# Two attention products in quarters of the TensorE array, with the projection's columns laid out by graph

## The chip, the cores and the metric

The kernel runs on one core of one Trainium2 chip. The metric is the device time of one execution in microseconds (us): the median over several runs, lower is better. "The profiled execution" is one run with the hardware profiler on; its trace gives every instruction on every engine with start and duration.

The engines are TensorE (PE in the profile; its weight loads are listed apart as PEld), VectorE (DVE), ScalarE (ACT), GpSimd (POOL) and the one that issues most loads (SP). Each works through its own queue in order.

## The reference

Two layers, each of a graph attention and a mixture of experts, on 128 graphs of 64 nodes with 256 features, all in float32:

```
x, adj: (128, 64, 256), (128, 64, 64)
for layer in (0, 1):
    h  = layernorm(x)                       # per node
    Wh = h @ W                              # 256 x 256, per node
    e  = (Wh @ a1)[:, :, None] + (Wh @ a2)[:, None, :]     # 64 x 64 per graph
    if layer == 1: e = where(e > 0, e, 0.2 * e)
    att = softmax(where(adj > 0, e, -9e15), axis=-1)
    x  = x + elu(att @ Wh)                  # att is 64 x 64, Wh 64 x 256, per graph
    x  = x + moe(layernorm(x))              # 8 experts, each node goes to 2
```

The attention never crosses from one graph to another. What the change touches is how `e` and `att @ Wh` are formed.

## The kernel before

**Blocks.** The 8192 nodes are cut into 16 blocks of 512 rows. A block is 4 tiles (`TT`) of 128 rows, and a tile holds 2 graphs of 64 nodes (`NG`) on the 128 partitions. There are 16 blocks in each of the two layers, so the attention, the generator `attend` (L303 to L423), runs 32 times.

**One block's attention.** Layer norm is applied by ScalarE (`xn`, L278). TensorE transposes `xn` into two PSUM tiles (`pt`, L289), which go to SBUF as `xt`. For each of the 4 tiles TensorE multiplies `xt` with the weights (`pw`, L334, 258 columns: 256 of `Wh` and the two scores `Wh @ a1`, `Wh @ a2`), and ScalarE copies the result to `wh` (L345). VectorE spreads the second score on a diagonal (`sm2`, L349). Then come the two products of this study:

- `pe` (L357, L358): two products of 128x128 by 128x256 into one PSUM tile. `same` is a constant 128x128 matrix with ones in the two 64x64 diagonal blocks, so that it sums `sm2` within each graph; the identity adds the first score.
- `po` (L402): for each of the 4 tiles one product of 128x128 by 128x256. The stationary side `pT` is the transposed attention, which is zero outside its two 64x64 diagonal blocks. Two tiles share one PSUM bank: tiles 0 and 1 in `po[0]`, tiles 2 and 3 in `po[1]`.

Between the two, VectorE adds the mask (L374; in layer 1 ScalarE copies `pe` out first, L368, and VectorE applies the leaky part, L371), and takes the maximum; ScalarE takes the exponentials (L380), VectorE divides (L387), TensorE transposes the 4 tiles of the attention to 64 partitions (`pp`, L391), and VectorE and ScalarE each copy one half of `pp` into one of three constant buffers `pT_bd`, which were set to zero once at the start (L170 to L172, L394, L396). After `po`, ScalarE takes `exp` of it (`ex`, L411), and VectorE forms the elu and the residual sum (L417, L420).

**PSUM.** All of `pt`, `pw`, `pe`, `pp` and `po` come from one pool with two banks in turn (tag `"a"` of `ps_c`). The router has two banks (tag `"r"`), and the experts four (tag `"hy"`).

**The experts.** `route` (L459) sorts rows into lists in DRAM by indirect DMA (L573). The experts work on slots of 256 rows read back from the lists: `px` (L878, transposes), `xT` (L883, VectorE copy), `ph` (L960), `hT` (L970, ScalarE), `py` (L993), `ys` (L1004), and an indirect DMA out (L1026, L1036).

**Order.** From block 3 on, nothing is left to a scheduler: the instructions of TensorE, VectorE, ScalarE and SyncE stand in the order in which the Python program issues them. The strings `STEPS` (L34) are that order written out by hand, one for each layer. A token advances one generator by one `yield`: `a1` is the attention of the next block, `r0` the router of the present one, `x0`, `h0`, `y0` the phases of an expert slot. The places of the `yield`s in `attend` therefore decide what stands between two of its instructions. In `po`'s loop there are four yields: after the products of `po[0]`, after its `exp`, after the products of `po[1]`, after its `exp`. In layer 0 the products of `po[0]` and `po[1]` follow each other on TensorE; in layer 1, from its second block on, the transposes `px` of an expert slot stand between them, and in its blocks 1 to 6 (counted from 0) the `ph` of that same slot comes next.

A float32 product shows in the trace as two pairs of LDWEIGHTS and MATMUL records on the same operands, one pair after the other; a transpose shows as one pair.

Of the kernel before, what the change touches and what calls it, by code (L numbers as in the profile page):

```python
# [16 lines left out]
P = 128  # L17
# [33 lines left out]
def adj_ffn_kernel(  # L51
# [89 lines left out]
    nc.gpsimd.tensor_tensor(imod, ident[:, 0:NG], ident[:, NG : 2 * NG], ALU.add)  # L141
    same = const.tile([P, P], F32, name="same")
    nc.gpsimd.memset(same, 0.0)
    for g in range(2):
        r = slice(g * NG, (g + 1) * NG)
        nc.gpsimd.memset(same[r, r], 1.0)
    nhalf = const.tile([P, TT], F32, name="nhalf")
# [21 lines left out]
    nc.gpsimd.memset(pad[:, :, META + 1 : META + 2], -1.0)  # L169
    pT_bd = [const.tile([P, TT, P], F32, name=f"pT_bd{i}") for i in range(3)]  # L170
    for t in pT_bd:
        nc.gpsimd.memset(t, 0.0)  # L172

# [107 lines left out]

    def transposed(src, tag, ptag, name, both):

        xt = work.tile([P, KD, TB], F32, tag=tag, name=f"xt_{name}", bufs=2)
        pts = []
        for k in range(KD):
            pt = ps_c.tile([P, TB], F32, tag=ptag, name=f"pt_{name}_{k}")
            for t in range(TT):
                nc.tensor.transpose(  # L289
                    pt[:, t * P : (t + 1) * P], src[:, t, k * P : (k + 1) * P], ident  # L290
                )
            pts.append(pt)
            yield
        for k, pt in enumerate(pts):
# [4 lines left out]
            else:  # L299
                nc.scalar.copy(xt[:, k, :], pt)  # L300
        return xt

    def attend(l, b, blk):  # L303
# [22 lines left out]
        yield 1  # L326
        xt = yield from transposed(xn, "xt", "a", name, l == 0 and b < FIRST)
        yield 1
        wh = work.tile([P, TT, D + 2], F32, tag="wh", name=f"wh_{name}")
        pws = []  # L330
        for t in range(TT):
# [23 lines left out]
        yield 1  # L355
        pe = ps_c.tile([P, TT, NG], F32, tag="a", name=f"pe_{name}")
        nc.tensor.matmul(pe, lhsT=same, rhs=sm2, start=True, stop=False)  # L357
        nc.tensor.matmul(  # L358
            pe,
            lhsT=ident,  # L360
            rhs=wh[:, :, D : D + 1].to_broadcast([P, TT, NG]),
            start=False,
            stop=True,
        )
        yield
        ee = work.tile([P, TT, NG], F32, tag="ee", name=f"ee_{name}")
        if l == 1:
            nc.scalar.copy(ee, pe)  # L368
        yield
        if l == 1:  # L370
            nc.vector.scalar_tensor_tensor(ee, ee, ALPHA, ee, ALU.mult, ALU.max)  # L371
            nc.vector.tensor_tensor(ee, ee, m, ALU.add)
        else:
            nc.vector.tensor_tensor(ee, pe, m, ALU.add)  # L374
        mx = small.tile([P, TT], F32, tag="emx", name=f"emx_{name}")
# [16 lines left out]
        yield  # L392
        pT = pT_bd[(NB * l + b) % 3]
        nc.vector.tensor_copy(pT[0:NG, :, 0:NG], pp[:, :, 0:NG])  # L394
        yield
        nc.scalar.copy(pT[NG:P, :, NG:P], pp[:, :, NG:P])  # L396
        yield 1
        po, ex = [], []
        for h in range(TT // 2):
            po.append(ps_c.tile([P, 2, D], F32, tag="a", name=f"po_{name}_{h}"))  # L400
            for j in range(2):
                nc.tensor.matmul(  # L402
                    po[h][:, j, :],
                    lhsT=pT[:, 2 * h + j, :],
                    rhs=wh[:, 2 * h + j, 0:D],
                    start=True,
                    stop=True,
                )
            ex.append(work.tile([P, 2, D], F32, tag="ex", name=f"ex_{name}_{h}"))
            yield  # L410
            nc.scalar.activation(ex[h], po[h], AF.Exp)  # L411
            yield 1 if h == TT // 2 - 1 else None
        xb = work.tile([P, TT, D], F32, tag="xb", name=f"xb_{name}")
        blk["xb"] = xb
        rs = [slice(2 * h, 2 * h + 2) for h in range(TT // 2)]
        for h, r in enumerate(rs):
# [872 lines left out]
```

## Time and profile before

| | |
|---|---|
| median of 6 runs | 1336.43 us (1333.05 to 1343.47) |
| the profiled execution | 1334.46 us, of which the instructions span 1332.7 us |
| granted TensorE clock, mean over the span | 0.955 |
| instructions in the trace | 22375 |
| MATMUL records of `pe` (L357 and L358) | 64 and 64 |
| MATMUL records of `po` (L402) | 256 |
| MATMUL records of `pp` (L391) | 128 |

How to read it: the profile page gives the busy time of each engine over the whole span, then the chain of work that ended last, followed back from the last instruction (an engine's share of that chain is the share of the span in which this engine's work was what the end waited for). The view by stages gives the busy time of each engine in stretches of the span. The timeline lists instructions by engine in order of time, those of one line merged: start, time covered, engine, line, output and inputs, the array's rows and columns in use (`128*128`), the moving side (`128x256`), and the count. A MATMUL's end is modelled (its pipeline included), so the time that one really takes of TensorE is read from the distance between the starts of neighbours, not from the duration.

### The profile page before, as it was taken

What the parts mean: (1) busy time and instruction counts of PE and PEld (TensorE: products, weight loads), DVE (VectorE), ACT (ScalarE), POOL (GpSimd) and SP (SyncE); (2) the same over time, 40 slices, a digit from 0 to 9 for tenths busy, and PEclk for the clock granted to TensorE, in tenths of its full rate; (3) what the DMA queues carried; (4) which work ended last, traced back from release to release, by engine and by line L of the source; (5) the groups of instructions that cost most, each with busy time, mean ns of one, the idle gap of its engine ahead of it and who ended that gap; (6) DMA issues with size and microseconds to landing.
All of it is one profiled execution on the core that took longest, in us unless ns stands there. A gap on an engine that the chain in (4) does not pass through costs nothing.

```text
span 1332.7 us, 22375 instructions
## 1 busy us (share of the span) xinstructions
PE 1198.6 (90%) x6240; PEld 1030.7 (77%) x6240; DVE 861.6 (65%) x3477; ACT 661.2 (50%) x1562; POOL 716.8 (54%) x697
## 2 busy tenths in 40 slices
PE   6867898989888889899899899999999999988992
PEld 4655787868777777688788788888888888877981
DVE  3756777777676787888777477766677754332330
ACT  5745565656666665466454445454545453323330
POOL 4173656656655566466554565566565556533233
PEclk9868999998999999899999999999999999989996
DMA  8636667778876877899897887889988778899963
GB/s 235 207 107 195 218 209 247 223 233 261 274 222 200 290 251 252 274 294 302 280 265 212 241 254 225 234 244 277 289 243 232 179 203 243 225 271 282 276 151 35
DMA packets 275116, 311.69 MB, mean 234 GB/s; under 512 B 40615, under 2 KB 236334, under 8 KB 274992
## 3 DMA queue, kind: packets, MB, share of 16 engines
q1 hardware_dynamic: 219552, 225.02, 54.1%
q0 software_dynamic: 38544, 68.46, 20.2%
q10 hardware_dynamic: 16896, 16.78, 3.7%
q8 instruction: 50, 0.82, 0.2%
q14 instruction: 74, 0.61, 0.1%
HBM read 212.25 MB, written 99.75 MB: 234 GB/s over the span
## 4 chain that ended last, share of the span: by engine, by line
PE 58%; DVE 17%; DMA 7%; issue 4%; ACT 3%; SPq 3%; POOL 2%; POOLq 0%; DVEq 0%; ACTq 0%
PE ph_s L960 20%; PE py_s L993 18%; PE pw_g L334 7%; PE pl_r L478 3%; PE px_s L878 3%; DVE ys_s L1004 2%; PE po_g L402 2%; DMA lists<-pad 2%; DVE xT_s L883 2%; DMA out_dram<-ys_s,to_s 1%; PE pt_r L289 1%; PE pt_g L289 1%; DMA res<-ys_s,to_s 1%; ACT xn_g L278 1%; DMA wc_s<-in_w_dram 1%
## 5 line engine op out<-in xcount | busy, mean ns | idle before, releaser
L960 PE MATMUL ph_s<-xT_s,wc_s 128*128 128x256 f32 (+1 forms) x1760 | 395.9, 377 | 19.8 <-DVE xT_s L883 10.9
L993 PE MATMUL py_s<-wc_s,hT_s 128*128 128x256 f32 x1648 | 386.7, 384 | 10.1 <-ACT hT_s L970 10.0
L960 PEld LDWEIGHTS ph_s<-xT_s,wc_s 128*128 128x128 f32 x1760 | 324.8, 197 | 67.4 <-DVE xT_s L883 15.9
L573 POOL DMA_INDIRECT lists<-tn_r,ix_r x256 | 252.4, 986 | 179.8 <-issue 87.6
L993 PEld LDWEIGHTS py_s<-wc_s,hT_s 128*128 128x128 f32 x1648 | 307.3, 192 | 51.8 <-ACT hT_s L970 13.6
L1036 POOL DMA_INDIRECT out_dram<-ys_s,to_s x135 | 213.6, 1582 | 238.6 <-DMA out_dram<-ys_s,to_s 89.8
L970 ACT ACTIVATE hT_s<-ph_s,wc_s 128x256 f32<-128x256 f32 (+1 forms) x440 | 174.0, 455 | 131.8 <-PE ph_s L960 84.1
L1026 POOL DMA_INDIRECT res<-ys_s,to_s x142 | 143.2, 1008 | 61.0 <-issue 22.7
L1004 DVE TENSOR_TENSOR ys_s<-py_s,wc_s 128x512 f32<-128x512 f32 (+1 forms) x149 | 96.2, 650 | 88.3 <-PE py_s L993 75.3
L334 PE MATMUL pw_g<-gw,xt_g 128*128 128x258 f32 x512 | 128.4, 401 | 15.2 <-DVE to_s L895 7.2
L883 DVE COPY xT_s<-px_s 128x512 f32<-128x512 f32 (+1 forms) x140 | 95.1, 680 | 63.8 <-PE px_s L878 62.5
L1059 ACT ACTIVATE ys_s<-ys_s,cf_s 128x256 f32<-128x256 f32 x135 | 61.1, 500 | 140.4 <-DVE ys_s L1004 140.4
L334 PEld LDWEIGHTS pw_g<-gw,xt_g 128*128 128x128 f32 x512 | 96.9, 197 | 40.7 <-ACT wh_g L345 9.8
L278 ACT ACTIVATE xn_g<-xs,nb_g,rs_g 128x256 f32<-128x256 f32 x128 | 67.2, 591 | 103.1 <-DVE nb_g L272 103.1
L878 PE MATMUL px_s<-ident,xg_s 128*128 128x128 f32 x554 | 84.5, 277 | 8.6 <-DMA xg_s<-lists 8.6
L349 DVE TENSOR_TENSOR sm_g<-imod,wh_g 128x256 f32<-128x256 f32 x32 | 13.6, 425 | 114.3 <-ACT wh_g L345 114.2
L402 PE MATMUL po_g<-wh_g,pT_bd 128*128 128x256 f32 x256 | 73.4, 425 | 13.2 <-ACT pT_bd L396 12.5
L878 PEld LDWEIGHTS px_s<-ident,xg_s 128*128 128x128 f32 x554 | 69.4, 147 | 19.0 <-DVE hat_p_15r L710 5.2
L278 ACT ACTIVATE tn_r<-xb_g,nb_r,rs_r 128x256 f32<-128x256 f32 x128 | 66.7, 589 | 33.1 <-DVE nb_r L272 26.5
L345 ACT COPY wh_g<-pw_g 128x258 f32<-128x258 f32 x128 | 47.6, 374 | 59.3 <-PE pw_g L334 58.7
L289 PE MATMUL pt_g<-ident,xn_g 128*128 128x128 f32 x256 | 49.8, 312 | 26.3 <-ACT xn_g L278 20.5
L269 POOL TENSOR_TENSOR rs_r<-ve_r,nhalf 128x4 f32<-128x4 f32 x32 | 34.2, 1068 | 69.9 <-DVE ve_r L266 39.1
(501 smaller groups left out, 1601.8 us busy)
## 6 DMA issues: line engine op xcount, KB each, us to landing
wc_s<-in_w_dram SPq DMA_DIRECT2D x142, 512.0 KB
wc_s<-in_w_dram SPq DMA_DIRECT2D x156, 256.0 KB
xg_s<-lists SPq DMA_DIRECT2D x64, 260.0 KB
xg_s<-lists SPq DMA_DIRECT2D x64, 258.0 KB
yb<-res SPq DMA_DIRECT2D x16, 1024.0 KB
wc_s<-bcat SPq DMA_DIRECT2D x78, 129.0 KB
wc_s<-bcat SPq DMA_DIRECT2D x71, 130.0 KB
xs<-in_x_dram SPq DMA_DIRECT2D x16, 512.0 KB
```

Source lines behind the costliest of these rows:

```text
L278: nc.scalar.activation(outs(t), xb[:, t, :], AF.Identity, bias=nb[:, t : t + 1], scale=rs[:, t : t + 1])
L334: nc.tensor.matmul(pw, lhsT=xt[:, k, t * P : (t + 1) * P], rhs=gw[l][:, k, :], start=(k == 0), stop=(k == KD - 1),)
L402: nc.tensor.matmul(po[h][:, j, :], lhsT=pT[:, 2 * h + j, :], rhs=wh[:, 2 * h + j, 0:D], start=True, stop=True,)
L573: ins = pooled(f"lists{l}", lambda: nc.gpsimd.indirect_dma_start(out=lists[l], out_offset=bass.IndirectOffsetOnAxis(ap=ix[:, k, t : t + 1] ...
L878: nc.tensor.transpose(px[:, c, t * P : (t + 1) * P], xg[:, t, c * P : (c + 1) * P], ident)
L883: nc.vector.tensor_copy(xT[:, :, 0 : st * P], px[:, :, 0 : st * P])
L960: nc.tensor.matmul(ph[:, j, r], lhsT=w[:, o : o + P], rhs=xT[:, c, r], start=(c == 0), stop=(c == KD - 1),)
L970: nc.scalar.activation(hT[:, f + j, r], ph[:, j, r], AF.Gelu if l == 0 else AF.Relu, bias=w[:, OB1[l] + f + j : OB1[l] + f + j + 1],)
L993: nc.tensor.matmul(py[:, t, :], lhsT=hT[:, f, t * P : (t + 1) * P], rhs=w[:, O2[l] + f * D : O2[l] + (f + 1) * D], start=(f == 0), stop=(f ...
L1004: nc.vector.tensor_tensor(ys[:, r, :], py[:, r, :], w[:, OB2[l] : OB1[l]].unsqueeze(1).to_broadcast([P, r.stop - r.start, D]), ALU.add,)
L1026: ins = pooled(group, lambda: nc.gpsimd.indirect_dma_start(out=res[sl["part"]], out_offset=self.row(sl, t), in_=sl["ys"][:, t, :], in_offs ...
L1036: ins = pooled("sums", lambda: nc.gpsimd.indirect_dma_start(out=out, out_offset=self.row(sl, t), in_=sl["ys"][:, t, :], in_offset=None, co ...
```

## The change

`pe` and `po` are computed graph by graph, as 64x64 products, each in one quarter of the TensorE array: the row half `q` holds the contraction, the column half `j` the output partitions. For that the 64 rows of a graph must lie on the row half on which the product contracts, so the columns of `xt`, and with them the rows of `wh` and `sm2`, are laid out anew: partition half `q` and tile `2h + j` now hold graph `j` of the original tile `2h + q`. The layout is made where the transposes `pt` write to PSUM (two runs of 64 columns instead of one of 128). The outputs `pe`, `po` come back in the original layout.

- `same` and its three fills go, and `pT_bd` with its three fills; `pT` becomes an ordinary work tile of half the size.
- `pe`: 8 products of 64x64 by 64x128 in place of 2 of 128x128 by 128x256, into two PSUM tiles, one for each row half `q`.
- `po`: 8 products of 64x64 by 64x256 in place of 4 of 128x128 by 128x256, into two PSUM tiles, one for each `q`. All 8 stand ahead of the first `yield`, where before the second half stood two yields later. The number of yields is the same.
- The quarters are taken in the order (0,0), (1,1), (0,1), (1,0) of (`q`, `j`).
- What reads `pe` is cut in two: in layer 1 the copy of ScalarE, in layer 0 the mask addition of VectorE. `exp`, the elu and the sum are over tiles `q`, `q + 2` instead of `2h`, `2h + 1`, in as many instructions as before.

TensorE has 4041 matrix instructions (a float32 product counted once) after the change, against 3721; ScalarE and VectorE have 16 more each, GpSimd 6 fewer. In the hand-ordered part the only move is that of `po`'s second half to ahead of `px` in layer 1; in the first three blocks, which a scheduler orders, the quarters of `pe` and `po` stand in other orders too.

```diff
@@ constants @@
-    same = const.tile([P, P], F32, name="same")
-    nc.gpsimd.memset(same, 0.0)
-    for g in range(2):
-        r = slice(g * NG, (g + 1) * NG)
-        nc.gpsimd.memset(same[r, r], 1.0)
...
-    pT_bd = [const.tile([P, TT, P], F32, name=f"pT_bd{i}") for i in range(3)]
-    for t in pT_bd:
-        nc.gpsimd.memset(t, 0.0)
@@ transposed @@
                 nc.tensor.transpose(
-                    pt[:, t * P : (t + 1) * P], src[:, t, k * P : (k + 1) * P], ident
+                    cols(pt, t) if cols else pt[:, t * P : (t + 1) * P],
+                    src[:, t, k * P : (k + 1) * P],
+                    ident,
                 )
+    def by_graph(v, t):
+
+        return v.rearrange("p (h j q n) -> p h q j n", h=TT // 2, q=2, j=2)[:, t // 2, t % 2, :, :]
+
+    QUADS = [(0, 0), (1, 1), (0, 1), (1, 0)]
+
+    def half(q):
+        return slice(q * NG, (q + 1) * NG)
@@ attend @@
-        xt = yield from transposed(xn, "xt", "a", name, l == 0 and b < FIRST)
+        xt = yield from transposed(xn, "xt", "a", name, l == 0 and b < FIRST, by_graph)
...
-        pe = ps_c.tile([P, TT, NG], F32, tag="a", name=f"pe_{name}")
-        nc.tensor.matmul(pe, lhsT=same, rhs=sm2, start=True, stop=False)
-        nc.tensor.matmul(
-            pe,
-            lhsT=ident,
-            rhs=wh[:, :, D : D + 1].to_broadcast([P, TT, NG]),
-            start=False,
-            stop=True,
-        )
+        pe = [ps_c.tile([P, TT // 2, NG], F32, tag="a", name=f"pe_{name}_{q}") for q in range(2)]
+        for i in range(2):
+            for q, j in QUADS:
+                r = half(q)
+                nc.tensor.matmul(
+                    pe[q][half(j), :, :],
+                    lhsT=(ident if i else ones)[r, r],
+                    rhs=(
+                        wh[r, j::2, D : D + 1].to_broadcast([NG, TT // 2, NG])
+                        if i else sm2[r, j::2, :]
+                    ),
+                    start=(i == 0),
+                    stop=(i == 1),
+                )
         yield
         ee = work.tile([P, TT, NG], F32, tag="ee", name=f"ee_{name}")
         if l == 1:
-            nc.scalar.copy(ee, pe)
+            for q in range(2):
+                nc.scalar.copy(ee[:, q::2, :], pe[q])
...
-            nc.vector.tensor_tensor(ee, pe, m, ALU.add)
+            for q in range(2):
+                nc.vector.tensor_tensor(ee[:, q::2, :], pe[q], m[:, q::2, :], ALU.add)
...
-        pT = pT_bd[(NB * l + b) % 3]
-        nc.vector.tensor_copy(pT[0:NG, :, 0:NG], pp[:, :, 0:NG])
-        yield
-        nc.scalar.copy(pT[NG:P, :, NG:P], pp[:, :, NG:P])
+        pT = work.tile([P, TT // 2, P], F32, tag="pT", name=f"pT_{name}", bufs=2)
+        nc.vector.tensor_copy(pT[half(0), :, :], pp[:, 0::2, :])
+        yield
+        nc.scalar.copy(pT[half(1), :, :], pp[:, 1::2, :])
         yield 1
-        po, ex = [], []
+        po = [ps_c.tile([P, TT // 2, D], F32, tag="a", name=f"po_{name}_{q}") for q in range(2)]
+        ex = []
         for h in range(TT // 2):
-            po.append(ps_c.tile([P, 2, D], F32, tag="a", name=f"po_{name}_{h}"))
-            for j in range(2):
+            for q, j in QUADS:
                 nc.tensor.matmul(
-                    po[h][:, j, :],
-                    lhsT=pT[:, 2 * h + j, :],
-                    rhs=wh[:, 2 * h + j, 0:D],
+                    po[q][half(j), h, :],
+                    lhsT=pT[half(q), h, half(j)],
+                    rhs=wh[half(q), 2 * h + j, 0:D],
                     start=True,
                     stop=True,
                 )
-            ex.append(work.tile([P, 2, D], F32, tag="ex", name=f"ex_{name}_{h}"))
-            yield
-            nc.scalar.activation(ex[h], po[h], AF.Exp)
-            yield 1 if h == TT // 2 - 1 else None
+        yield
+        for q in range(2):
+            if q:
+                yield
+            ex.append(work.tile([P, TT // 2, D], F32, tag="ex", name=f"ex_{name}_{q}"))
+            nc.scalar.activation(ex[q], po[q], AF.Exp)
+            yield 1 if q else None
...
-        rs = [slice(2 * h, 2 * h + 2) for h in range(TT // 2)]
+        rs = [slice(q, TT, 2) for q in range(2)]
```

More of the change, by code (lines that the diff above doesn't have):

```diff
@@ L280, in ln_apply, with transposed @@
             )
-    def transposed(src, tag, ptag, name, both):
+    def transposed(src, tag, ptag, name, both, cols=None):
         xt = work.tile([P, KD, TB], F32, tag=tag, name=f"xt_{name}", bufs=2)
```

## The prediction

> **What bounds the kernel now.** I read the page first: busy times, then the chain of work that ended last.
>
> ```profile
> PE 1198.6 (90%) x6240; PEld 1030.7 (77%) x6240; DVE 861.6 (65%) x3477; ACT 661.2 (50%) x1562; POOL 716.8 (54%) x697
> ...
> PE 58%; DVE 17%; DMA 7%; issue 4%; ACT 3%; SPq 3%; POOL 2%; POOLq 0%; DVEq 0%; ACTq 0%
> ```
>
> TensorE is the bound: busy for 90% of the span and itself 58% of the chain. How tight it is where attention runs, the view by stages tells (columns: stage, its length, busy time of PE, PEld, DVE, ACT, POOL with counts, clock, DMA share, GB/s):
>
> ```profile
> 300.00:500.00 200.00, 175.60 (x942) 149.44 (x943) 145.21 (x579) 123.94 (x263) 116.51 (x116) 0.97 0.78 250
> ...
> 900.00:1100.00 200.00, 199.84 (x1059) 176.25 (x1058) 140.08 (x561) 98.27 (x255) 117.59 (x94) 1.00 0.83 237
> ```
>
> In layer 0 (first stage) TensorE is busy 88%, late in layer 1 100%. The stages between lie between these, and the mean over the 32 blocks is about 0.92. So I count 0.92 of any TensorE time that the attention gains or loses.
>
> What the two products cost comes from the distance between starts in the timeline of TensorE late in layer 1, where nothing waits:
>
> ```profile
> 1077.63 0.60 PE L357 MATMUL pe_g<-sm_g,same 128*128 128x256 f32 x2
> 1078.07 0.59 PE L358 MATMUL pe_g<-wh_g,ident 128*128 128x256 f32 x2
> 1078.50 1.89 PE L960 MATMUL ph_s<-xT_s,wc_s 128*128 128x256 f32 x8
> 1080.23 1.85 PE L478 MATMUL pl_r<-rw,xt_r 128*128 128x8 f32 x16
> 1081.93 3.70 PE L993 MATMUL py_s<-wc_s,hT_s 128*128 128x256 f32 x16
> 1085.47 0.60 PE L878 MATMUL px_s<-ident,xg_s 128*128 128x128 f32 x4
> 1085.90 0.60 PE L391 MATMUL pp_g<-ident,ee_g 128*64 128x128 f32 x4
> 1086.34 3.62 PE L993 MATMUL py_s<-wc_s,hT_s 128*128 128x256 f32 x16
> 1089.80 1.03 PE L402 MATMUL po_g<-wh_g,pT_bd 128*128 128x256 f32 x4
> 1090.66 0.60 PE L878 MATMUL px_s<-ident,xg_s 128*128 128x128 f32 x4
> 1091.10 1.03 PE L402 MATMUL po_g<-wh_g,pT_bd 128*128 128x256 f32 x4
> 1091.96 7.07 PE L960 MATMUL ph_s<-xT_s,wc_s 128*128 128x256 f32 x32
> ```
>
> Four things: `pe` takes 1078.50 - 1077.63 = 0.87 us for 4 records, and `po` twice 0.86 us for 4, so 0.215 us for a record with 256 moving columns. A record with 128 takes 0.108 (`px`, `pp`: 0.43 for 4). A record with 8 takes (1081.93 - 1080.23)/16 = 0.106: there the weight load of 128 columns is the limit. And `pp`, which uses 64 columns of the array, follows and precedes 128-column work at the same distance as any other.
>
> The last view is the start of `pe` in layer 0 after an idle stretch, with the weight loads:
>
> ```profile
> 125.46 0.30 PEld L357 LDWEIGHTS pe_g<-sm_g,same 128*128 128x128 f32 x2 [0.28 <-DVE sm_g L349]
> 125.47 0.70 PE L357 MATMUL pe_g<-sm_g,same 128*128 128x256 f32 x2
> 126.00 0.59 PE L358 MATMUL pe_g<-wh_g,ident 128*128 128x256 f32 x2
> ```
>
> Two records take 0.53 us here instead of 0.43: an uncovered load of 128 columns costs 0.10 us. Elsewhere it hides behind the record before.
>
> **The change part by part.** Before, a block pays 0.87 + 1.72 = 2.59 us for the two products, 82.9 us in 32 blocks; this is all the change can win from.
>
> *The quarter products.* After, there are 8 products in `pe` with half the moving columns and 8 in `po` with the same. A float32 product is two records, one after the other, in the same quarter, and all MATMULs in the trace start in program order. End to end that is 16 x 0.108 = 1.73 us for `pe` and 16 x 0.215 = 3.44 us for `po`: exactly twice as much. Quarter products use a quarter of the array each, so the edit only pays if several run side by side. The trace of before has none that could, so I bound it. Four abreast: 5.17/4 = 1.29 us, a gain of 1.30 us for a block (41.6 us in all). None abreast: a loss of 2.58 us (82.6 us).
>
> Between them I take what order allows. The second record of a product needs its own quarter, which the first still uses; so it waits, and the next product's first record stands behind it. Once it starts, that next record can start beside it in another quarter, and no third one can. So neighbours overlap in pairs, and n products take n + 1 record times instead of 2n: 9 x 0.108 + 9 x 0.215 = 2.91 us, already 0.32 more than before. To it comes the weight load of the next product, if it too starts only with the record ahead of it. By columns (64 of the 128 that cost 0.106) I estimate 0.053 us; the ends are 0 (hidden) and 0.106. For 7 handovers in each of `pe` and `po` that is 14 x 0.053 = 0.74 us. I keep it, since every load that follows an unfinished record in this trace hides behind one record only. Sum 3.65 us, a loss of 1.06 us for a block, 33.9 in all, and 31.2 us after the factor 0.92.
>
> *Switching between full array and quarters*, 4 times in a block: the only change of form in the trace, into and out of `pp`, costs nothing (0.43 and 0.44 us for 4 records on both sides). I take 0. The upper end is a pipeline that must run empty each time: the modelled duration of a 256-column record (median 0.379 us in the view of `po`) less its 0.215 is 0.164 us, 128 times, 21 us.
>
> *`po`'s second half ahead of `px`.* In layer 1 `px` stands between the halves, and its copy by VectorE hides behind the second half. This row is from the block shown:
>
> ```profile
> 1091.30 0.69 DVE L883 COPY xT_s<-px_s 128x512 f32<-128x512 f32 x1 [0.21 <-PE px_s L878]
> ```
>
> From the end of `px` (1091.10) to the end of the copy (1091.99) is 0.89 us, and the second half covers 0.86 of them. After, `px` comes after all of `po`, and where its own `ph` is next, in blocks 1 to 6 of layer 1, TensorE stands still for those 0.89 us: 6 x 0.89 = 5 us. In the later blocks another slot's `ph` of 16 records stands between, and it is hidden.
>
> *Readers of `pe` cut in two.* ScalarE's copies take 0.372 us for 256 columns and 0.58 for 512, so 0.27 for 128: twice that is 0.17 more, 16 times, in an engine with 50% idle in front of work that VectorE continues; 0. VectorE's mask addition takes 0.42 for 256 and 0.68 for 512 columns, so 0.29 for 128, 0.16 more, 16 times, 2.5 us on an engine that is 17% of the chain and mostly so in layer 0; I take 1 us. Without cover the two together cost 5 us.
>
> *`exp` of the first half* waits for all of `po`; ScalarE's next work that TensorE waits for is behind a later `ph`, so 0. *PSUM*: `pe` takes both `"a"` banks instead of one. Their last contents are `pw` of tiles 2 and 3, which ScalarE has read before `sm2` can start; no new wait. *Start*: six fills leave POOL (some 2 us), but its first work after them waits for a load of `adj`; 0. *Transposes in two runs of 64*: same columns, 0.
>
> *Sum*: 31.2 + 5 + 1 = 37 us on the profiled execution's 1334.5, so 1371.5; that execution is 2 us under the median of the runs, and I predict 1371 us.
>
> The Trainium skill, page "TensorEngine Tiling (Array Packing)", section "Key Properties", says that changing the tiling mode drains TensorE. For a change of columns alone the `pp` rows disagree; by the rule the result would be some 21 us later, 1392. Page "TensorE: Matmul & The Clock Gate", section "Part 3: Packing small matmuls — row/col tiling", has products in different tiles start about 4 ns apart and sixteen of them run 10.6 times as fast; by that alone four would run abreast and the result would be near 1302. No run here shows it, and it speaks of tiles, not of products of two records each.
>
> **The rivals.**
>
> *Four abreast (faster).* One mechanism: the second record of a product waits in its quarter without holding up the next quarters. Then `pe` and `po` cost 1.29 us, and 41.6 x 0.92 = 38 us go, less the 6 us of the other edits: 1302. It decides once the two products take under 2.4 us for a block. For it: the operands are independent and the outputs lie in different banks or partitions. Against it: in this trace no MATMUL ever starts before the one ahead of it in the program.
>
> *End to end (slower still).* Float32 products in quarters don't overlap at all: 82.6 x 0.95 (TensorE is then the bound nearly throughout) = 78, plus 6: 1419; with switches that run empty 1440. For it: not one pair of products in the trace runs side by side.
>
> *Pairs, all loads hidden*: 0.32 x 32 x 0.92 + 6 = 15 us, 1350; part of my forecast's own range of 1345 to 1392. *Balance*: some three abreast, whose gain the other edits eat; within 7 us of now.
>
> **How the numbers follow.** Pairs (1345 to 1392) 0.41; end to end 0.32; four abreast 0.20; balance 0.07. A change under 0.5%, 6.7 us, can't be told from none. So faster 0.20, same 0.07, slower 0.73. The range leaves out the faster case and holds the rest: 1330 to 1440.
>
> **What would show it.** The distance from the first `pe` record to what follows late in layer 1: 1.34 us for pairs, 0.43 for four abreast, 1.73 end to end (0.87 before); for `po` 2.3, 0.86 and 3.4 (1.72 before). Starts of different quarters in pairs, or all apart. A gap in front of `ph` after `px` in blocks 1 to 6 of layer 1. A gap of some 0.16 us at `pe`'s and `po`'s edges, if switching costs. The forecast is wrong if more than two records share a start, or none do.

## The result and the profile after

The change makes the kernel slightly slower: 1347.6 us (median of 20 runs, 1339.54 to 1354.73) against 1336.1 us (46 runs) on the same chip, ratio 1.0078 with a 95% interval of 1.0062 to 1.0093. Run again on another chip it gave 1.0054 (1.0036 to 1.0072). The profiled execution spans 1341.3 us, 8.6 more than before. The sign was forecast and the size was not (37 us), and the reasons turn out to be mostly others.

The page of the changed kernel, the busy times and the shares of the chain:

```profile
PE 1188.3 (89%) x6880; PEld 997.3 (74%) x6880; DVE 863.0 (64%) x3493; ACT 659.3 (49%) x1578; POOL 715.0 (53%) x691
...
PE 48%; DVE 28%; DMA 5%; ACT 5%; issue 4%; POOL 2%; SPq 1%; POOLq 0%; DVEq 0%; ACTq 0%
```

TensorE is busy 10 us less, and its share of the chain falls from 58% to 48%, while VectorE's rises from 17% to 28%. So TensorE has less to do, and the end waits for something else more often. The view by stages of the changed kernel (columns as before):

```profile
300.00:500.00 200.00, 172.32 (x1037) 143.08 (x1036) 145.48 (x576) 118.48 (x256) 115.52 (x115) 0.94 0.79 251
900.00:1100.00 200.00, 199.27 (x1182) 171.48 (x1180) 142.82 (x575) 98.92 (x262) 121.54 (x97) 1.00 0.82 238
```

In layer 0 TensorE is busy 86% instead of 88%, at a granted clock of 0.94 instead of 0.97. Late in layer 1 it is full as before. There the timeline of TensorE shows what the products cost now:

```profile
1059.40 1.09 PE L412 MATMUL po_g<-wh_g,pT_g 64*64 64x256 f32 x16
1060.42 0.66 PE L891 MATMUL px_s<-ident,xg_s 128*128 128x128 f32 x4
1060.92 7.07 PE L973 MATMUL ph_s<-xT_s,wc_s 128*128 128x256 f32 x32
...
1086.53 0.60 PE L281 MATMUL pt_r<-ident,tn_r 128*128 128x128 f32 x4
1087.06 0.45 PE L363 MATMUL pe_g<-sm_g,ones 64*64 64x128 f32 x8
1087.33 0.40 PE L363 MATMUL pe_g<-wh_g,ident 64*64 64x128 f32 x8
1087.65 1.99 PE L973 MATMUL ph_s<-xT_s,wc_s 128*128 128x256 f32 x8
1089.49 1.85 PE L491 MATMUL pl_r<-rw,xt_r 128*128 128x8 f32 x16
```

By the distance between starts, `po` takes 1060.42 - 1059.40 = 1.02 us (1.72 before) and `pe` 1087.65 - 1087.06 = 0.59 (0.87 before). This is neither pairs nor end to end: four quarters run abreast. The starts of the 16 MATMUL records of that `po`, one by one (us from the span's start):

```
1059.398  .405  .412  .418
1059.665  .672  .678  .685
1059.881  .890  .897  .901
1060.097  .105  .112  .117
```

Bunches of four, 4 to 9 ns apart, and the bunches 0.216 us apart (0.267 for the first). The semaphores in the trace tell which records these are: the first weight load of the first bunch waits for VectorE's copy of `pT` (row half 0), the second already for ScalarE's (row half 1), though in the program the second record of the first product stands between them. So the second record of a float32 product waits for its own quarter, and the products of the other quarters pass it. In block 17 one record starts 0.18 us ahead of three others, and the four records of its quarter keep that lead (535.69, 535.96, 536.17 and 536.39 us, against 535.87, 536.14, 536.35 and 536.57).

The switch between the two forms is not free. Four bunches at 0.215 would be 0.86 us, `po` takes 0.16 more; `pe`, with bunches at 0.108, also takes 0.16 more than 0.43. And the neighbours are late: `pt_r` 0.53 instead of 0.43, `ph` 1.84 instead of 1.73, `px` 0.50 instead of 0.43, and `py` ahead of `po` 3.55 instead of 3.46. Together some 0.69 us in a block, 0.17 for each of the four changes of form. (What happens inside TensorE at such a change the trace doesn't show.) What remains is (0.87 + 1.72) - (0.59 + 1.02) - 0.37 = 0.61 us a block, 20 us in 32 blocks, that TensorE wins (0.37 is what the neighbours lose). The question is where they went.

**Where it is lost and won.** I compare when `pe` of each block starts (blocks 0 to 15 are layer 0), in us after the same block in the profile of before. Single executions of one kernel differ by some 3 us here, so the table gives several: A are the profiles with quarters in both layers (the changed kernel twice), B those with layer 0 as before and quarters in layer 1, C those with quarters in layer 0 alone. They are explained below.

| kernel | block 4 | 16 | 17 | 23 | 31 |
|---|---|---|---|---|---|
| A changed | 2.3 | 6.9 | 7.6 | 13.9 | 9.4 |
| A changed, again | 3.8 | 10.1 | 8.3 | 14.4 | 10.0 |
| B layer 1 alone | 2.4 | 4.4 | 2.6 | 8.7 | 4.1 |
| C layer 0 alone | 6.2 | 7.2 | 8.0 | 8.3 | 8.4 |
| C layer 0 alone, again | 5.4 | 8.8 | 9.7 | 9.8 | 9.9 |

Three parts can be read off. Layer 0 loses some 6 us: block 16 is 8 us late on average in the four profiles with quarters there, and 2 us (-0.8 to 4.8) in the five with layer 0 as before. Blocks 17 to 22 lose 6 us, where layer 1 has quarters. And blocks 23 to 31 win 4.5 us, 0.55 in a block, close to the 0.61 on paper: there TensorE is busy all the time.

### The profile page after: what moved, and what is told of

Same layout as the page of the kernel before. It is cut to its first block, busy times and chain, and to the rows that moved or that the text cites. A ratio compares the mean times of both kernels' runs of the same rounds, so it can differ in the third digit from the quotient of the medians.

```text
span 1341.3 us, 23677 instructions
## 1 busy us (share of the span) xinstructions
PE 1188.3 (89%) x6880; PEld 997.3 (74%) x6880; DVE 863.0 (64%) x3493; ACT 659.3 (49%) x1578; POOL 715.0 (53%) x691
## 4 chain that ended last, share of the span: by engine, by line
PE 48%; DVE 28%; DMA 5%; ACT 5%; issue 4%; POOL 2%; SPq 1%; POOLq 0%; DVEq 0%; ACTq 0%
PE ph_s L973 17%; PE py_s L1006 14%; PE pw_g L337 7%; DVE ys_s L1017 3%; PE pl_r L491 3%; DVE xT_s L896 3%; DVE xs L313 2%; ACT xn_g L270 2%; PE px_s L891 2%; PE pt_g L281 2%; DVE st_g L255 2%; DVE st_r L255 2%; DMA out_dram<-ys_s,to_s 1%; DVE xb_g L433 1%; DVE xb_g L430 1%
## 5 line engine op out<-in xcount | busy, mean ns | idle before, releaser
L973 PE MATMUL ph_s<-xT_s,wc_s 128*128 128x256 f32 (+1 forms) x1760 | 402.4, 381 | 29.9 <-DVE xT_s L896 20.5
L261 POOL TENSOR_TENSOR rs_r<-ve_r,nhalf 128x4 f32<-128x4 f32 x32 | 34.2, 1068 | 72.9 <-DVE ve_r L258 37.8
L281 PEld LDWEIGHTS pt_g<-ident,xn_g 128*128 128x128 f32 x256 | 33.5, 156 | 49.1 <-ACT xn_g L270 42.0
```

Of the source, the lines that this page charges most:

```text
L281: nc.tensor.transpose(cols(pt, t) if cols else pt[:, t * P : (t + 1) * P], src[:, t, k * P : (k + 1) * P], ident,)
L973: nc.tensor.matmul(ph[:, j, r], lhsT=w[:, o : o + P], rhs=xT[:, c, r], start=(c == 0), stop=(c == KD - 1),)
```

## The experiments

The runs fell on different chips: on some the kernel before takes 1336 to 1338 us, on others 1407 to 1416. Every ratio is against the kernel before on the same chip, with its 95% interval.

### First round: what of the change costs by itself

*Kernel before with both halves of `po` ahead of the first yield* (`e1`):

```diff
                     stop=True,
                 )
+        yield
+        for h in range(TT // 2):
+            if h:
+                yield
             ex.append(work.tile([P, 2, D], F32, tag="ex", name=f"ex_{name}_{h}"))
-            yield
             nc.scalar.activation(ex[h], po[h], AF.Exp)
```

> The kernel before, with both halves of po put ahead of the first yield, so that px comes after all of po in layer 1, as in the changed kernel; full-array products as before. Theory A (the move costs: ph waits for the copy xT): 5 to 10 us slower than before (1341 to 1346), since in the changed kernel TensorE's wait in front of ph for xT rose from 10.9 to 20.5 us. Theory B (the clock: TensorE is granted half speed for 144.6 us instead of 123.0, because shorter products leave it idle more often) says no change from this edit, within 3 us. Theory C (the readers of pe cut in two cost DVE and ACT time) says no change either.

Measured: 1.0027 (0.9995 to 1.006), where the kernel before takes 1416 us. That fits the 5 us of the prediction (0.35%), but the interval does not exclude zero.

*Kernel before with the readers of `pe` cut in two* (`e2`):

```diff
-            nc.scalar.copy(ee, pe)
+            for q in range(2):
+                nc.scalar.copy(ee[:, q::2, :], pe[:, q::2, :])
...
-            nc.vector.tensor_tensor(ee, pe, m, ALU.add)
+            for q in range(2):
+                nc.vector.tensor_tensor(ee[:, q::2, :], pe[:, q::2, :], m[:, q::2, :], ALU.add)
```

> The kernel before, with the reader of pe cut in two instructions as in the changed kernel (ScalarE's copy in layer 1, VectorE's mask addition in layer 0); full-array products as before. Theory C: 3 to 5 us slower than before, 0.16 us for each of 32 blocks with nothing to cover it. Theories A and B: within 2 us of before.

Measured: 1.0049 (1.0017 to 1.0081), some 7 us: far more than the 1 us that I had put on it. This is the first surprise, and the third round takes it up.

*The changed kernel with `px` ahead of `po` in layer 1* (`e3`), a token moved in `STEPS[1]` (a part of the line):

```diff
-y1 y2 a1 x2 r0 x0 x1 a1 p R1
+y1 y2 x2 r0 x0 a1 x1 a1 p R1
```

> The changed kernel with one token moved in the order of layer 1, so that px stands ahead of po there too and the copy xT hides behind po. Theory A: 5 to 10 us faster than the changed kernel, so 1338 to 1343, about level with before, and TensorE's wait for xT in front of ph back to about 11 us. Theories B and C: within 3 us of the changed kernel's 1347.6.

Measured: 1.0186 (1.014 to 1.0232). On this chip the loss lies almost wholly in layer 0, which this edit leaves alone: block 16 starts at 579.9 us, in `e2` at 551.0, and from there to block 31 it is 609.6 us against 610.2. So the ratio says nothing of layer 1; the second round repeats the edit without quarters in layer 0.

*The changed kernel with filler products* (`e4`): one of 128x128 by 128x512 ahead of `pt` and one ahead of `po`, in blocks 4 to 22. The lines show the one ahead of `po`; the other stands in `transposed`.

```diff
+        if NB * l + b in FILL:
+            nc.tensor.matmul(po[0], lhsT=ident, rhs=gw[0][:, :, 0:D], start=True, stop=True)
```

> The changed kernel with two products added in each of blocks 4 to 22 (identity by 512 columns, 0.86 us of TensorE each), whose result is overwritten by the work that follows: one ahead of the transposes pt of the attention, one ahead of po, where TensorE waits in layer 0. Theory B: time at half clock falls from 144.6 us towards 120, and the kernel is 3 to 8 us faster than the changed one. Theories A and C: no faster; 0 to 30 us slower, by how much of the 38 products' 33 us meets an idle TensorE.

Measured: 1.0374 (1.0329 to 1.0419). Half clock means windows of 3.4 us and more in which the trace gives TensorE a granted clock of 0.5. Between blocks 4 and 16 TensorE spends 106 us in such windows instead of 133 in `e3`, and yet the stretch takes 478.8 us instead of 475.5. The kernel is not faster, as theory B had it; but the 24 fillers of this stretch are 20.6 us of work, of which only 3.3 show, so the run cannot tell what the clock is worth.

### Second round: layer by layer

A flag chooses quarters or the old form block by block; in both, the copies of `pp` go to the diagonal blocks of `pT_bd`.

```diff
+    def in_quads(l, b):
+        return l == 1
...
+        quads = in_quads(l, b)
```

The changed kernel (`e5`), quarters in layer 1 alone (`e6`), in layer 0 alone (`e7`), and in layer 1 alone with the token moved as above (`e8`):

> The changed kernel once more, so that it stands on the same chip as the other kernels of this call. Ratio to the kernel before 1.008 where the kernel before takes 1336 us, and up to 1.02 on a chip where it takes 1416. Theory A (what is lost lies where TensorE waits for other engines, layer 0 and the first blocks of layer 1; what is won lies from block 23 on): relative to the kernel before, block 16 starts about 7 us late or more, and blocks 23 to 31 win 0.5 us each. Theory B (half clock): TensorE spends some 20 us more at half clock than before.

> Quarters in layer 1 alone; layer 0 as before. Theory A (the loss of layer 0 comes from quarters where TensorE has slack, the loss of blocks 16 to 22 from the order in layer 1): block 16 level with before, blocks 16 to 22 lose some 7 us, blocks 23 to 31 win 4.5 us: 2 us slower, ratio 1.002 (0.998 to 1.006). Theory B (TensorE with less to do falls to half clock more often, all over the kernel): time at half clock as before up to block 16, so again level there, then less than 3 us lost in blocks 16 to 22. Theory R (the loss is the per-block price of the readers cut in two and of switching, alike in both layers): half of the loss of the changed kernel, ratio 1.004 to 1.01.

> Quarters in layer 0 alone; layer 1 as before. Theory A: block 16 starts as late as in the changed kernel (7 us, up to 30 on a slower chip), and the delay stays level to the end; ratio 1.005 (up to 1.02). Theory B: the same lateness, and time at half clock 15 us or more above the kernel before in the first 500 us. Theory R: half of the loss of the changed kernel. If layer 0 costs nothing here, ratio 1.000, the loss of the changed kernel is all in layer 1.

> Quarters in layer 1 alone, and there px ahead of po, so that po stands between px and the ph that waits for the copy of px. Theory A: blocks 16 to 22 lose 0 to 2 us instead of 7 and the later blocks win 4.5: ratio 0.996 (0.993 to 1.000), faster than before and than the changed kernel. Theory B: the order makes no difference, ratio as with quarters in layer 1 alone. Theory R: 1.003.

Measured, all on one chip: both layers 1.0054 (1.0036 to 1.0072); layer 1 alone 1.0004 (0.9984 to 1.0024); layer 0 alone 1.0063 (1.004 to 1.0086); layer 1 with `px` ahead 0.9975 (0.9957 to 0.9993). The parts add up, and theory A stands: the loss is in layer 0, and layer 1 is a draw of a loss and a gain. Theory R, half and half, is out. The last is the first version below both kernels, by 0.25%; run again on another chip (`e13`, below) its interval includes 1.

Why does layer 1 lose in its first blocks? One reason is the wait that was forecast. The view of TensorE's waits in the stretch from 480 to 760 us, before and after (us in total, times, longest):

```profile
PE ph_s L960 <- DVE xT_s L883: 4.3, 2, 2.6
```

```profile
PE ph_s L973 <- DVE xT_s L896: 10.0, 8, 2.7
```

That is 5.7 us more. But VectorE's queue shows that the place of `px` is only half of it. In block 17 of the kernel before, the copy `xT` stands behind the copy of `pT` and a row of small router instructions, and ends 3.2 us after that copy began:

```profile
526.32 0.41 DVE L394 COPY pT_bd<-pp_g 64x256 f32<-64x256 f32 x1
...
528.79 0.69 DVE L883 COPY xT_s<-px_s 128x512 f32<-128x512 f32 x1
```

So it does in the changed kernel (3.3), and in `e8` too (3.1), where `px` is done more than a microsecond sooner after that start. Before, `po`, `px` and `po` filled this time; now `po` is 0.7 us shorter, and what it saves becomes a wait. With `px` ahead of `po` that `ph` still waits 0.99 us, and the waits in this stretch are 7.6 us (6 times).

### Third round: the table load

The other reason is on ScalarE. Block 19 in the kernel before, ScalarE and then VectorE's maximum:

```profile
593.53 0.37 ACT L368 COPY ee_g<-pe_g 128x256 f32<-128x256 f32 x1 [0.28 <-PE pe_g L358]
593.92 1.28 ACT L380 ACT_TABLE_LOAD   x1
595.31 0.35 ACT L380 ACTIVATE ee_g<-ee_g,emx_g 128x64 f32<-128x64 f32 x1
```

```profile
594.85 0.42 DVE L376 TENSOR_REDUCE emx_g<-ee_g 128x4 f32<-128x256 f32 x1
```

The exponentials need another table in ScalarE, and its load of 1.28 us runs while VectorE adds the mask and takes the maximum. The first exponential starts 0.03 us after the maximum. The same block in the changed kernel:

```profile
603.67 0.43 ACT L377 COPY ee_g<-pe_g 128x128 f32<-128x128 f32 x2
605.67 1.28 ACT L390 ACT_TABLE_LOAD   x1 [1.57 <-DVE emx_g L386]
606.96 0.35 ACT L390 ACTIVATE ee_g<-ee_g,emx_g 128x64 f32<-128x64 f32 x1
```

```profile
605.17 0.42 DVE L386 TENSOR_REDUCE emx_g<-ee_g 128x4 f32<-128x256 f32 x1
```

Now the load itself waits for the maximum, and the first exponential starts 1.37 us after it. So it is in all of blocks 16 to 21, in all ten profiles that have the copy of `pe` cut in two without more; in the kernel before it is 0.03 to 0.04 us in blocks 17 to 21 and 0.43 in block 16. In the trace a separate semaphore wait stands ahead of the load, which the kernel before does not have: the wait that used to sit on the exponential now sits in front of its table load. From block 22 on no table is loaded there, and the exponentials start 0.09 us after the maximum.

The Trainium skill, page "ScalarE: Activation LUTs", section "What ACT_TABLE_LOAD costs", gives some 1283 ns for the load, as here, and some 1380 ns more for a drain; the rows here show no such gap, neither ahead of the load (593.92, after a copy that ends at 593.90) nor behind it (606.96, after a load that ends at 606.95).

To test it, one small exponential on a constant goes behind the copies, in blocks 0 to 5 of layer 1, so that the load comes with an instruction that waits for nothing (`e9`, and `e14` with its partner `e13`, which is `e8` again):

```diff
                 for q in range(2):
                     nc.scalar.copy(ee[:, q::2, :], pe[q])
+                if b < 6:
+                    nc.scalar.activation(early, imod[:, 0:1], AF.Exp)
```

> Quarters in layer 1 alone with px ahead of po, and in blocks 0 to 5 of layer 1 one small exp of 128x1 on a constant behind the two copies of pe, so that ScalarE's table load for exp need not stand behind the wait for the maximum. Theory T (cutting the copy of pe in two gives the exponentials one more wait, which stands ahead of the table load of 1.28 us; before, the load ran beside VectorE's mask and maximum): in the six blocks the first exp starts 0.1 to 0.3 us after the maximum, not 1.37; six times 1.1 to 1.3 us, 6 to 8 us, come back, block 23 starts level with before or earlier, and the whole takes some 1326 us where the kernel before takes 1337, ratio 0.992 (0.989 to 0.995). Rival (the loss of blocks 16 to 22 is the clock or the waits for xT): no change against the kernel without the small exp, ratio 0.9975.

> Quarters in layer 1 alone with px ahead of po, once more, as partner of the kernel with the early table load. Ratio to the kernel before 0.9975 as measured (0.996 to 0.9995).

> The same with the small exp of 128x1 behind the copies of pe in blocks 0 to 5 of layer 1. Theory T (the table load of 1.28 us behind the wait for the maximum costs 1.1 to 1.3 us in each of the six blocks): 5 to 8 us below its partner, ratio to the kernel before 0.993 where that takes 1337 us; block 23 starts 2 to 4 us earlier than in the kernel before. Rival (the table load is hidden by other waits): within 2 us of its partner.

Block 19 with the early load:

```profile
595.76 0.43 ACT L403 COPY ee_g<-pe_g 128x128 f32<-128x128 f32 x2
596.22 1.28 ACT L405 ACT_TABLE_LOAD   x1
597.51 0.20 ACT L405 ACTIVATE early<-imod 128x1 f32<-128x1 f32 x1
597.79 0.35 ACT L423 ACTIVATE ee_g<-ee_g,emx_g 128x64 f32<-128x64 f32 x1
```

The load runs beside VectorE again. `e9`: 0.9985 (0.9959 to 1.001), on a chip where the kernel before takes 1413 us. `e13`: 0.9988 (0.9963 to 1.0012); `e14`: 0.9962 (0.994 to 0.9985), a second version that is faster than before, 1332.5 us against 1337.8. Of the 5 to 8 us expected between the partners only some 2 to 4 came, and the two intervals overlap; the profiles say why. From block 17 to 23 the partner loses 3.3 us and the kernel with the early load wins 0.8: 4.1 us back in five loads. But block 16 gives 3.6 us away, so that these two profiles differ by 0.3 us from block 16 to 23. There the small exponential with its load stands in front of the copy `xt_r` (the wait of `pl` for it is 2.21 us instead of 0.71), and the `pl` and `py` behind that wait run at half clock:

```profile
484.46 3.16 PE L552 MATMUL pl_r<-rw,xt_r 128*128 128x8 f32 x14 [2.21 <-ACT xt_r L304]
487.47 3.68 PE L1067 MATMUL py_s<-wc_s,hT_s 128*128 128x256 f32 x8
```

Eight records of `py` take 3.5 us here, where they take 1.81 in the partner. That the longer wait brings on the half clock is not shown. Leaving the small exponential out of that block was not tried.

Each cut alone in the kernel before, as in `e2`:

> The kernel before with only the mask addition of layer 0 cut in two. Two additions over 128 columns take 0.13 us more than one over 256 (0.29 each against 0.42, overlapping a little): 16 times 0.13 is 2 us if all of it lies on the path, ratio 1.000 to 1.0015. If it is what layer 0 loses with quarters, 1.005.

> The kernel before with only ScalarE's copy of pe of layer 1 cut in two. Theory T: the table load comes behind the wait for the maximum in blocks 0 to 5 of layer 1, the first exp starts 1.37 us after the maximum in place of 0.03, and the kernel loses 5 to 8 us, all of it between block 16 and block 23, ratio 1.005 (1.003 to 1.006). Rival (the added 0.17 us of copy is all there is, hidden): 1.000.

Measured, on a chip where the kernel before takes 1407 us: the mask addition of layer 0 cut 0.9968 (0.9921 to 1.0014), the copy of layer 1 cut 1.0037 (0.9995 to 1.0078). The load stands behind the wait in the second and not in the first. The size in layer 1 is near the expected one, though its interval touches none; in layer 0 the cut costs nothing that shows, and more than some 2 us is outside the interval. Added, the two give 1.0005, where both together gave 1.0049 on another chip (`e2`); the intervals overlap.

### Four records of a quarter in a row

*The changed kernel with `po` ordered by quarter* (`e12`), two products of a quarter one after the other:

```diff
-        for h in range(TT // 2):
-            for q, j in QUADS:
+        for q, j in QUADS:
+            for h in range(TT // 2):
```

> The changed kernel with po's products ordered by quarter, two products of a quarter one after the other, then the next quarter. Theory of four queues (each quarter has its own, a product that waits in its quarter holds up no other, however many stand behind it): po stays at 1.02 us late in layer 1. Theory of the prediction, one product further on (whatever waits behind a product of its own quarter holds up all that follow): the second product of a quarter waits for the two records of the first, and neighbours overlap only across the change of quarter: 1.5 to 3 us. If only the second record of the same product can wait aside: some 1.9 to 2.6 us.

```profile
1060.65 1.11 PE L412 MATMUL po_g<-wh_g,pT_g 64*64 64x256 f32 x16
1061.70 0.66 PE L891 MATMUL px_s<-ident,xg_s 128*128 128x128 f32 x4
```

1061.70 - 1060.65 = 1.05 us against 1.02 (1.04 in most blocks). Four records of one quarter in a row hold up the others by next to nothing: within a bunch the starts are 10 to 16 ns apart instead of 4 to 9. So what waits for its quarter does not stand in the way of what follows: the assumption of the prediction is refuted for four records deep. Whether each quarter has a queue of its own the trace does not tell.

This kernel ran once, 1462 us on a chip where the kernel before takes 1413, so only its rows are used. One of them limits what was said of layer 1: from block 16 to 23 it takes 313.5 us, and `e9`, with `px` ahead and the early load, 287.8 on the same chip; on the faster chips the changed kernel takes 281.3 there and `e8` 277.1. So where the chip is slower, layer 1 in the changed kernel's order can lose much more than 6 us; no run separates the causes.

### Layer 0

*Quarters in blocks 4 to 15 of layer 0 alone* (`e10`), *the same with each product of `po` done twice* (`e11`), and, on another chip, *quarters in all of layer 0 with 0.86 us of filler ahead of `po`* (`e15`) beside its partner (`e16`, which is `e7` again). The three edits, in that order:

```diff
-        return l == 0
+        return l == 0 and b >= 4
...
-            for h in range(TT // 2):
+            for h in [*range(TT // 2)] * 2:
...
+            if b >= 4:
+                for _ in range(2):
+                    nc.tensor.matmul(po[0][:, 0, :], lhsT=ident, rhs=gw[0][:, 0, 0:D], start=True, stop=True)
```

> Quarters in blocks 4 to 15 of layer 0 alone. Theory S (part of the loss of layer 0 arises in blocks 0 to 3, where a scheduler orders the work and pe needs two of the banks at a time, part in blocks 4 to 8): some 3 us of the 8 are gone, ratio 1.003 to 1.004, and blocks 4 to 8 still lose some 1.4 us each. Theory B (half clock): the same, with the windows of half clock in blocks 5 and 6 on ph instead of po. Rival (all of it is the readers of pe cut in two, 0.16 us in a block on VectorE): 12 times 0.16, ratio 1.0015.

> Quarters in blocks 4 to 15 of layer 0 alone, and there each product of po is done twice, one after the other into the same place, so that TensorE is as busy with po as before (some 2.0 us in place of 1.0; 1.72 before). The doubled work is left in on purpose. Theory B (VectorE sets the pace of layer 0; with less to do TensorE waits longer and falls to half clock later, on the ph that VectorE and ScalarE wait for): the windows of half clock go back onto po, and the 1.4 us a block of blocks 4 to 8 are gone: faster than with each product once, ratio 1.000 to 1.002. Rival (the clock has no part): as with each product once, or slower by up to 12 times 1.0 us, ratio 1.003 to 1.013.

> Quarters in layer 0 alone, and in its blocks 4 to 15 two products of 128x128 by 128x256 more, 0.86 us, ahead of po, where TensorE waits 1.7 us or more for the copy of pT; their result is written over by po. Theory B (half clock on ph is what costs): the windows of half clock go back onto po, time at half clock on ph falls by 5 us or more, and the kernel is 2 to 5 us faster than its partner where the kernel before takes 1337 us, 5 to 15 us where it takes 1413. Rival (the clock only goes along with a loss that has another cause): within 1.5 us of its partner, or slower, whatever the clock does.

> Quarters in layer 0 alone, once more, as partner. Ratio to the kernel before 1.0063 where that takes 1337 us, 1.015 to 1.02 where it takes 1413.

Measured where the kernel before takes 1413 us: `e10` 1.0148 (1.011 to 1.0187), `e11` 1.0171 (1.0136 to 1.0206). Where it takes 1338: `e15` 1.0097 (1.0066 to 1.0129), `e16` 1.0056 (1.0028 to 1.0084).

Part of the loss comes before block 4. On the slower chips the seven profiles without quarters in these blocks start block 4 at 95.5 to 99.5 us, and the three with them (`e3`, `e4`, `e12`) at 102.7 to 108.9. On the faster ones five profiles with quarters start it on average 4.0 us after before's profile (2.3 to 6.2), and the five with layer 0 as before (its own among them) 1.5 (-0.6 to 4.1): some 2.5 us. The distance from block 0 to block 2 is clearer: 20.2 us in all twelve profiles without quarters there, 21.6 to 23.0 in the eight with them. In these blocks a scheduler orders the work: in `e7` all but two records of `pe` in block 0 wait 0.45 us for a copy of ScalarE that frees a bank, and in block 2 other work stands between the halves of `pe`. How much of the loss that makes is not shown.

The other 3.5 us (more on the slower chips) can be placed on the faster chips, counting a block from the start of its `pe` to the next. In five profiles with layer 0 as before, block 5 takes 29.3 us and block 6 30.3; in four with quarters, 30.9 and 31.4 to 31.7. Block 15 takes 35.3 to 36.7 and 36.8 to 37.8. The rest of blocks 4 to 15 together loses nothing. In block 5 the windows of half clock do move, as theory B has it. Layer 0 as before (`e6`), then with quarters (`e7`):

```profile
135.81 3.68 PE L473 MATMUL po_g<-wh_g,pT_bd 128*128 128x256 f32 x8 [2.15 <-ACT pT_bd L467]
```

```profile
152.83 2.89 PE L1031 MATMUL ph_s<-xT_s,wc_s 128*128 128x256 f32 x8
```

In the first, half clock falls on `po` (8 records in 3.5 us), while VectorE was busy with other work without a gap; in the second on the next `ph` (2.7 us instead of 1.73), behind which ScalarE's copies for the next block wait. Profiles that share a program in the blocks compared suggest what such a window costs. Block 6 with layer 0 as before takes 30.3 us with a window on `po` and the `ph` behind it, and 30.3 without any window (`e14`). Block 15 takes 35.3 or 35.4 us without a window and 36.7 with one on `ph` and `py` (`e6`). From block 0 to 2, kernels with quarters take 21.6 us without a window and 22.8 to 23.0 with one. So 3.4 us at half clock cost nothing in one place and 1.2 to 1.4 us in another, and with quarters a window falls on `ph` in blocks 5 and 15, and in most profiles in block 6.

The two kernels that put TensorE's work back did not win, but they did not settle it either. `po` twice brought the time at half clock between blocks 4 and 16 from 143 to 109 us and the stretch, with the doubled products in it, from 475.6 to 473.3. The filler in `e15` did not move the windows: in blocks 5 and 6 they stay on `px` and `ph`, the blocks take 30.9 and 31.8 us as without it, and between blocks 4 and 16 half clock is 48 us against 41 in the partner. It cut the wait of `po` for `pT` from 8.4 to 4.8 us, so only 3.6 of its 10.3 us were hidden, and it cost the remaining 7. So TensorE's own time is on the path in much of layer 0, and still a shorter `pe` and `po` brought nothing there. Why the windows fall elsewhere with quarters, and what layer 0 would cost if they did not, stays open. The cut of the mask addition is ruled out by `e17` as a cause of more than some 2 us.

## Why the prediction was wrong, step by step

- **Pairs: wrong, the step that failed.** It took the queue to be held up by the second record of a product. The trace shows four abreast, and `e12` that even four records of one quarter don't hold up the rest. `pe` takes 0.59 us, not 1.34; `po` 1.02, not 2.31. With the switching below, TensorE wins 0.61 us in a block where a loss of 1.06 was counted. The rival "four abreast" named this mechanism; its time of 1302 us missed as well.
- **Switching at 0: wrong.** 0.69 us in a block, 0.17 a change; the upper end that was given, 0.164, was near the measured value. The row of `pp` that decided for 0 changes only the columns in use, and that costs nothing. Page "TensorEngine Tiling (Array Packing)", section "Key Properties", of the Trainium skill, which has a change of mode drain TensorE, fits the price for quarters; that it is a drain no run here shows.
- **The factor 0.92: wrong.** A stage where TensorE is busy 88% need not pay back 88% of what TensorE saves. The gain came through from block 23 on (4.5 us) and nowhere else.
- **`po` ahead of `px`, 5 us: right in place and near in size.** 5.7 us more of wait, in 6 more places; moving `px` back ahead won some 3 us. That VectorE's queue holds the copy `xT` up by itself was not in the prediction.
- **Readers of `pe`, 1 us: wrong.** The added time is smaller than counted, since the two halves overlap: two copies take 0.43 us against 0.37 for one, two mask additions 0.49 against 0.42. What was missed is that the cut moves a table load behind a wait: 4 us in the profile of `e14`, some 5 by `e18`, whose interval reaches zero. The 5 us "without cover" hit the size by chance, with another mechanism.
- **PSUM and start at 0: wrong by some 2.5 us together**, in the first four blocks, where the scheduler has to find two banks for `pe`; how the loss divides is not shown.
- **The clock: no term.** In layer 0 windows of half clock fall on work that nothing hides, and blocks 5, 6 and 15 are 1.3 to 1.6 us longer.
- **The last step of the sum:** 1371.5 is the profiled execution; with the 2 us named beside it the median would have been some 1373, not 1371.

So the forecast was slower for a wrong reason, and its sign came right by luck: a TensorE loss of 31 us was counted where TensorE wins 20 on paper, of which 4.5 come through. Against them stand some 6 us in blocks 17 to 22, where `px` and the table load explain most, and some 6 in layer 0. Layer 1 is even in the end, so what makes the kernel slower is layer 0, and there the loss is placed but its cause is not shown.

## What to carry to other kernels

Small float32 products in the four quarters of TensorE do run side by side, but each change of form costs some 0.17 us, so gathering quarter products should pay more than sprinkling them (not tried here). Before counting a gain, find out stage by stage whether the end waits for this engine alone; put the change only there. And when a reader is cut in two, look at what stands behind it on its engine: a table load that had been hidden can come out from behind a wait, and one small instruction ahead of it hides it again, if nothing urgent stands behind that one, as in block 16.

## What the runs showed of the hardware that I had not expected

- Float32 products of two records each run four abreast, starts 4 to 9 ns apart, and four records of one quarter in a row hold up the others by 0.02 us.
- Going from full array to quarters or back costs 0.17 us; using fewer columns alone, 0.
- ScalarE's table load of 1.28 us ran while the input of its exponential was still being made, until a separate wait stood in front of the load: the exponential then started 1.37 us after its input instead of 0.03.
- With a window of 3.4 us at half clock the same program took no longer in block 6, where it fell on `po` and the next `ph`, and 1.2 to 1.4 us longer in two other places.
- The same program takes 1336 to 1338 us on some chips and 1407 to 1416 on others. Where it takes 1413, quarters in blocks 4 to 15 alone cost 1.5% (`e10`); where it takes 1337 or 1338, quarters in all of layer 0 cost 0.6%.
